# A graph attention kernel: small operands and statistics of its list-making stage moved to PSUM, ScalarE and TensorE, and the order of rows found by a product instead of scatters

## The chip, the cores and the metric

The kernel runs on one core of a Trainium2 chip. The metric is the device time of one execution in microseconds (us), as the median of the runs shown. Engines are named as the profile names them: PE (TensorE), DVE (VectorE), ACT (ScalarE), POOL (GpSimd) and SP (SyncE, which here only issues transfers). SBUF is the memory on which the engines work, PSUM the small memory that PE writes its products to; DVE and ACT read and write both.

## The reference

The input is a matrix x of 3327 rows (nodes) by 1024, and an adjacency matrix of 3327 x 3327 int32 with ones on its diagonal and about 17 ones in a row, at random places.

```
h = relu(layernorm(x))                   # no gain, no bias, eps 1e-5
f = h @ Wf + bf;  g = h @ Wg + bg        # 1024 x 1024 weights, float32
e = relu(f @ g.T)
scores = where(adj > 0, e, -9e15)
out = x + softmax(scores, axis=1) @ (h @ W + bW)
```

## The kernel before

The function `edge_path` does all the work on the usual input; `dense_path` is a fallback behind a flag that is not taken. The rows are cut into NT = 26 tiles of 128, the last of 127. The work has two stages.

**Stage one, the making of lists** (lines 356 to 548, the loop at line 510). For each of the 26 tiles, `edges(t)` turns 128 rows of the adjacency matrix into 128 lists of at most KM = 40 neighbours:

- SP issues the load of the rows into tile `a` (L416; two buffers). ACT copies them to float in `r` and sums each row, which is the degree (L418; two buffers of `r`). POOL multiplies `r` by `iotaj`, the column numbers 1 to 3327 (L419).
- DVE takes the eight largest of each of 16 segments of 208 columns (MAX8, L422) into `cand`, counts them (L424), and draws the 40 largest from `cand` by five MAX8 and four MATCH_REPLACE (L429, L431). The result `lst` is clamped (L432) and written as int32 into its place in `pay` (L433), the table of lists, which has two more columns: the node's own number and its degree `dg` (L435, L436).
- DVE makes `oh`, a one-hot row of the degree over NBIN = 64 bins, by comparing `iotad` with `dg` (L437). For each node PE counts the earlier nodes of the same degree: a strictly triangular matrix `tri` times `oh` for those of the same tile (L439), and a matrix of ones `onesb` times `cum` for those of earlier tiles (L442). `cum` is the running sum of the `oh`, added on DVE (L443). DVE picks each node's own bin from the product (L448); this becomes `rp`.

`normed(t)` normalizes the same rows of x: load on SP (L395), BN_STATS on DVE (L398, L400), the square root on ACT (L402), reciprocal and the product `nmr` on DVE (L403, L405), one ACT pass for scale, shift and relu (L406), and a store of h to `hd` in device memory on SP (L407). Beside it the weights are folded into one matrix A = Wf Wgᵀ: tiles 0 to 7 load and transpose Wg (`load_Wg`, L457, L458), tiles 8 to 15 load and transpose Wf and make eight products of 16 matmuls of 512 columns (`make_A`, L482, 32 records of the trace each), with a bias row (L488). `make_rows` (L490 on), called at tile 16, makes the other bias rows, `v3` and `bW3`, which `split3` (L339) cuts into three bf16 parts on DVE, and the scalar `c_sb`.

After the loop DVE works out each node's rank by falling degree (L522 to L531): a running sum over the bins, a product over 1664 elements (L527), a sum. Then POOL issues 26 indirect scatters, which write the rows of `pay` to `pd` in device memory in the order of rank (L534).

**Stage two, attention** (L551 on), over 26 tiles of rows in the order of rank, so that all rows of a tile have nearly the same degree. `prepare(s)` loads the lists of tile s from `pd` into `pi` (SP, L597), POOL gathers the rows `hp` of h by the column of node numbers (line 599 through the helper at L566), PE transposes them and multiplies by A to `q` (L606), DVE makes the mask from the degrees (L610 to L613) and a bias `ci` (L616). For each neighbour k, POOL gathers the rows `G` of h (L566; 23 buffers) and DVE takes the dot product with `q` (L629). After the softmax, DVE and ACT sum the `G` with the weights into `y` (L667, L669), PE multiplies by W (L684), DVE adds x, gathered by POOL into `xp` (L693), and POOL scatters the rows to the output (L694). The degree cap of each tile (37 falling to 11) sets how many gathers and dots it has.

A scheduler of the framework decides in which order instructions stand on each engine, from its own estimates; every engine then runs its list in that order. A tile's buffers (a pool with `bufs=2`, say) decide how far one step can run ahead of the next.

## Time and profile before

| | before |
|---|---|
| median of 3 runs | 1936.72 us (1935.0 to 1939.14) |
| the profiled execution, own time | 1940.96 us |
| its span (first to last instruction) | 1939.2 us |
| mean granted TensorE clock | 0.803 of full speed |
| DVE busy | 1619.8 us (84%) |
| PE busy | 1069.0 us (55%) |
| POOL busy | 835.1 us (43%) |
| ACT busy | 258.8 us (13%) |

A row of a group of instructions reads: line, engine, operation, output<-input with the partitions x elements and the type, the count, then after the bar the busy time in us and the mean of one in ns, then the engine's idle time just ahead of them with what ended it. A row of a window reads: the stretch, its length, then the busy time of PE, PEld (PE's weight loads), DVE, ACT and POOL with the number of instructions, the granted clock of TensorE, the share of the DMA engines that was busy, and GB/s. A row of the timeline reads: start and duration in us, engine, line, operation, what is made from what, and in brackets the idle time ahead of it with what ended it. A row of the DMA issues reads: what is moved, the queue, the count, the KB of one, and the median time from issue to landing in us. SPq is the transfer queue that SP issues to, POOLq that of POOL.

### The profile page before, as it was taken

Reading aid. Unit: us, or ns where it says so; the run is one execution under the profiler, and the core shown is the slowest. Engines: PE = TensorE matmul, PEld = TensorE weight load, DVE = VectorE, ACT = ScalarE, POOL = GpSimd, SP = SyncE. Lnnn points to the kernel's source line nnn. Section 1 sums busy time; section 2 is a strip of 40 time slices with the busy share of each in tenths; the row PEclk is TensorE's granted clock in tenths of the full one; section 3 lists DMA queues with packets and bytes.
Section 4 is the critical chain, followed back from the end, with each engine's and each line's share of the span. In section 5 each row is a group of like instructions: output and inputs, shape, how many; then the busy total and the mean of one; then the engine's idle time right before and its main releaser. Section 6 shows DMA issues by size and latency. Waiting matters only on the chain.

```text
span 1939.2 us, 11080 instructions
## 1 busy us (share of the span) xinstructions
PE 1069.0 (55%) x2798; PEld 493.0 (25%) x2798; DVE 1619.8 (84%) x2880; ACT 258.8 (13%) x375; POOL 835.1 (43%) x624
## 2 busy tenths in 40 slices
PE   1117775500330472676645566677777678789463
PEld 0113342200110131233222223333333333334221
DVE  7999999634099999999998989889899898887680
ACT  2333434100000110011100000000000001001000
POOL 6445455114433544544335444444354454334610
PEclk9998887755665686887877788888888888899786
DMA  6556566100656857767467656556565565655620
GB/s 228 203 205 247 207 235 228 52 26 30 247 216 202 263 203 241 254 199 222 163 213 249 228 192 227 185 192 238 180 236 222 200 251 200 220 185 195 121 65 13
DMA packets 124618, 372.41 MB, mean 192 GB/s; under 512 B 41210, under 2 KB 41610, under 8 KB 121218
## 3 DMA queue, kind: packets, MB, share of 16 engines
q0 software_dynamic: 106288, 286.93, 43.6%
q1 hardware_dynamic: 18256, 84.68, 11.6%
q8 instruction: 24, 0.39, 0.1%
q14 instruction: 50, 0.40, 0.1%
HBM read 343.64 MB, written 27.81 MB: 192 GB/s over the span
## 4 chain that ended last, share of the span: by engine, by line
issue 24%; DVE 16%; PE 15%; DMA 10%; POOL 8%; ACT 1%; POOLq 0%; SPq 0%; DVEq 0%; ACTq 0%
DVE y L669 13%; PE ps_o L684 11%; POOL G L566 7%; DMA pi<-pd 3%; DMA G<-hd,pi 2%; DMA out_dram<-xp,pi 2%; PE ps_t L577 2%; PE q L606 1%; DMA hp<-hd,pi 1%; DVE junk L629 1%; DMA xp<-in_x_dram,pi 1%; PE ps_o L685 0%; ACT y L667 0%; DVE sc L629 0%; POOL out_dram L694 0%
## 5 line engine op out<-in xcount | busy, mean ns | idle before, releaser
L566 POOL DMA_INDIRECT G<-hd,pi x468 | 512.4, 1095 | 450.0 <-ACT y L667 172.9
L629 DVE CUSTOM_DVE_ANT_0 junk<-G,q,ci 128x1024 bf16<-128x1024 f32 (+1 forms) x468 | 597.7, 1277 | 35.4 <-PE q L607 22.1
L669 DVE SCALAR_TENSOR_TENSOR y<-G,sc,y 128x1024 f32<-128x1024 f32 (+1 forms) x442 | 566.4, 1283 | 26.1 <-ACT y L667 18.7
L684 PE MATMUL ps_o<-W_sb,yT 128*128 128x512 f32 (+1 forms) x832 | 408.4, 648 | 0.8 <-ACT yT L578 0.8
L606 PE MATMUL q<-A_sb,hT 128*128 128x512 f32 (+1 forms) x832 | 372.9, 601 | 7.0 <-ACT hT L578 7.0
L577 PE MATMUL ps_t<-ident,y 128*128 128x128 f32 (+1 forms) x208 | 48.9, 413 | 502.3 <-DVE y L669 283.3
L419 POOL TENSOR_TENSOR r<-r,iotaj 128x3327 f32<-128x3327 f32 (+1 forms) x26 | 187.4, 7209 | 229.8 <-ACT r L418 163.1
L684 PEld LDWEIGHTS ps_o<-W_sb,yT 128*128 128x128 f32 (+1 forms) x832 | 168.9, 209 | 210.2 <-issue 201.9
L606 PEld LDWEIGHTS q<-A_sb,hT 128*128 128x128 f32 (+1 forms) x832 | 154.5, 191 | 194.5 <-issue 180.5
L577 PEld LDWEIGHTS ps_t<-ident,y 128*128 128x128 f32 (+1 forms) x208 | 39.3, 217 | 509.4 <-issue 288.6
L482 PE MATMUL ps_A<-WgT,WfT 128*128 128x512 f32 x256 | 127.2, 660 | 14.6 <-ACT WfT L458 14.6
L694 POOL DMA_INDIRECT out_dram<-xp,pi x26 | 34.0, 1309 | 234.7 <-DVE xp L693 87.4
L439 PE MATMUL ps_pre<-oh,tri 128*128 128x64 bf16 x26 | 5.2, 203 | 230.1 <-DVE oh L437 216.6
L422 DVE MAX8 cand<-r 128x8 f32<-128x208 f32 (+2 forms) x416 | 122.4, 359 | 0.0
L578 ACT COPY yT<-ps_t 128x512 f32<-128x512 f32 (+1 forms) x52 | 30.1, 585 | 564.1 <-PE ps_t L577 563.9
L418 ACT ACTIVATE r<-a 128x3327 f32<-128x3327 int32 (+1 forms) x26 | 77.2, 2968 | 52.2 <-DMA a<-in_adj_dram 52.2
L693 DVE TENSOR_TENSOR xp<-ps_o,xp 128x512 f32<-128x512 f32 (+1 forms) x52 | 35.9, 690 | 47.3 <-PE ps_o L685 47.2
L610 DVE CAST df<-pi 128x1 f32<-128x1 int32 (+1 forms) x26 | 3.9, 150 | 85.2 <-DMA pi<-pd 85.2
L482 PEld LDWEIGHTS ps_A<-WgT,WfT 128*128 128x128 f32 x256 | 53.9, 214 | 82.3 <-issue 66.7
L578 ACT COPY hT<-ps_t 128x512 f32<-128x512 f32 (+1 forms) x52 | 28.0, 588 | 285.9 <-PE ps_t L577 225.0
L577 PE MATMUL ps_t<-ident,hp 128*128 128x128 f32 (+1 forms) x208 | 29.4, 286 | 63.6 <-DMA hp<-hd,pi 63.6
L566 POOL DMA_INDIRECT hp<-hd,pi x26 | 32.9, 1264 | 70.0 <-DMA pi<-pd 48.7
(115 smaller groups left out, 819.3 us busy)
## 6 DMA issues: line engine op xcount, KB each, us to landing
a<-in_adj_dram SPq DMA_DIRECT2D x25, 1663.5 KB, 8.7
xt<-in_x_dram SPq DMA_DIRECT2D x25, 512.0 KB, 4.8
hd<-xt SPq DMA_DIRECT2D x25, 512.0 KB, 3.0
G<-hd,pi POOLq DMA_INDIRECT x468, 5.9
wr<-in_L_gnn_Wg_dram SPq DMA_DIRECT2D x8, 512.0 KB, 7.6
wr<-in_L_gnn_Wf_dram SPq DMA_DIRECT2D x8, 512.0 KB, 5.2
W_sb<-in_L_gnn_W_dram SPq DMA_DIRECT2D x1, 4096.0 KB, 13.0
a<-in_adj_dram SPq DMA_DIRECT2D x1, 1650.5 KB
```

Source lines behind the costliest of these rows:

```text
L418: nc.scalar.activation(r[:n], a[:n], AF.Relu, accum_out=deg[:n, t : t + 1])
L419: nc.gpsimd.tensor_mul(r[:n], r[:n], iotaj[:n])
L422: nc.vector.max(cand[:n, s * 8 : s * 8 + 8], r[:n, s * SW : min(N, (s + 1) * SW)])
L482: nc.tensor.matmul(ps, WfT[:, k, :], WgT[:, k, o * CB : (o + 1) * CB], start=(k == 0), stop=(k == KD - 1))
L566: nc.gpsimd.indirect_dma_start(out=to, out_offset=None, in_=table, in_offset=bass.IndirectOffsetOnAxis(ap=idx, axis=0),)
L577: nc.tensor.transpose(ps[:, k, :n], of[:n, (g + k) * P : (g + k + 1) * P], ident[:n, :n])
L578: nc.scalar.copy(to[:, g : g + 4, :n], ps[:, :, :n])
L606: nc.tensor.matmul(qo, hT[:, k, :n], A_sb[:, k, o * CB : (o + 1) * CB], start=(k == 0), stop=False)
L629: nc.vector.tensor_tensor_reduce(junk[:n], g[:n], e["q"][:n], 1.0, e["ci"][:n], op0=ALU.mult, op1=ALU.add, accum_out=e["sc"][:n, k : k + 1],)
L669: nc.vector.scalar_tensor_tensor(y, G[s, k][:n], p, y, op0=ALU.mult, op1=ALU.add)
L684: nc.tensor.matmul(ps[:n], yT[:, k, :n], W_sb[:, k, o * CB : (o + 1) * CB], start=(k == 0), stop=False)
L693: nc.vector.tensor_add(xo, e["o"][o][:n], xo)
```

## The change

The change touches stage one, and the places where stage two takes the order of rows from. Line numbers here are those of the changed kernel. `p_c` and `p_lst` are pools in PSUM.

1. `iotad` and `lst` are placed in PSUM instead of SBUF.
2. The histogram is kept by PE: one PSUM tile `pre` is accumulated over the whole loop. For each tile PE adds `tri` times `oh` (L461), DVE reads its hit (L463 to L465), and then PE adds `low`, the lower triangle with its diagonal, times `oh` (L466), so that `pre` then holds in all rows the count of all tiles so far. `cum` and its additions go.
3. The statistics of the even tiles' layernorm are taken by ACT in two passes over x that sum (Copy and Square, L417, L421), those of the odd tiles by BN_STATS on DVE as before. `nmr` is made by ACT for all tiles. The stores of h to `hd` are issued by ACT instead of SP.
4. `edges` is cut in two: `degrees(t)` (load, L431, the ACT pass, L433, the POOL product, L434) now stands ahead of `normed(t)`, the rest after it.
5. The lists in `pay` lose the column of node numbers and are stored to `pd` in the order of nodes, in blocks of four tiles by plain stores on ACT's queue (`store_lists`, L471; the block of tiles t-7 to t-4 after tile t). Tiles 20 to 25 are stored after the loop, tile 25 with its 127 rows by a store of its own (L475).
6. After the loop, the rank is split in its low 7 bits and the rest, DVE makes a one-hot of each (`ohp` 128 x 26 x 128, `ohs`), and 26 matmuls add up `perm`: for each rank the number of the node that has it. The 26 scatters go.
7. In stage two `pi` is an indirect gather by POOL from `pd` with `perm` as its index, instead of a load by SP. `hp`, `xp` and the output scatter take their index from `perm` instead of a column of `pi`.
8. `make_rows` is called after the loop instead of at tile 16; its small loads are issued at the start.

```diff
-        iotad = c1.tile([P, NBIN], FP, name="iotad")
+        iotad = p_c.tile([P, NBIN], FP, name="iotad")
+        pre = p_c.tile([P, NBIN], FP, name="pre")
...
+            if t % 2:
...
+                nc.scalar.activation(nmr[:n], mv[:n, 0:1], AF.Copy, scale=-1.0)
+                nc.scalar.activation(rstd[:n], mv[:n, 1:2], AF.Sqrt, bias=eps[:n])
+            else:
+                nc.scalar.activation(j[:n], xt[:n], AF.Copy, accum_out=sums[:n, 0:1])
+                nc.scalar.activation(nmr[:n], sums[:n, 0:1], AF.Copy, scale=-1.0 / D)
+                nc.scalar.activation(j[:n], xt[:n], AF.Square, bias=nmr[:n], accum_out=sums[:n, 1:2])
+                nc.scalar.activation(rstd[:n], sums[:n, 1:2], AF.Sqrt, bias=eps[:n], scale=1.0 / D)
             nc.vector.reciprocal(rstd[:n], rstd[:n])
-            nc.vector.scalar_tensor_tensor(nmr[:n], mv[:n, 0:1], -1.0, rstd[:n], op0=ALU.mult, op1=ALU.mult)
+            nc.scalar.activation(nmr[:n], nmr[:n], AF.Copy, scale=rstd[:n])
             nc.scalar.activation(xt[:n], xt[:n], AF.Relu, bias=nmr[:n], scale=rstd[:n])
-            nc.sync.dma_start(hd[t * P : t * P + n, :], xt[:n])
+            nc.scalar.dma_start(hd[t * P : t * P + n, :], xt[:n])
...
-            lst = cpool.tile([P, KM], FP, name="lst")
+            lst = p_lst.tile([P, KM], FP, name="lst")
...
-            nc.tensor.matmul(ps, tri, oh[:, t, :], start=True, stop=(t == 0))
-                nc.tensor.matmul(ps, onesb, cum[t - 1], start=False, stop=True)
-                nc.vector.tensor_add(new, cum[t - 1], oh[:, t, :])
+            nc.tensor.matmul(pre, tri, oh[:, t, :], start=(t == 0), stop=False, skip_group_check=True)
             nc.vector.scalar_tensor_tensor(
-                hit[:n], ps[:n], 1.0, oh[:n, t, :], op0=ALU.mult, op1=ALU.mult, accum_out=rp[:n, t : t + 1]
+                hit[:n], pre[:n], 1.0, oh[:n, t, :], op0=ALU.mult, op1=ALU.mult, accum_out=rp[:n, t : t + 1]
             )
+            nc.tensor.matmul(pre, low, oh[:, t, :], start=False, stop=(t == NT - 1), skip_group_check=True)
...
         for t in range(NT):
-            edges(t)
+            r = degrees(t)
             normed(t)
+            edges(t, r)
+            if t % 4 == 3 and t > 4:
+                store_lists(t - 7, t - 3)
             if t < KD:
                 load_Wg(t)
             elif t < 2 * KD:
                 make_A(t - KD)
-            elif t == 2 * KD:
-                make_rows()
+        store_lists(20, NT)
...
+        nc.vector.tensor_tensor(
+            ohp, lo[:, :, None].to_broadcast([P, NT, P]), iotap[:, None, :].to_broadcast([P, NT, P]), op=ALU.is_equal
+        )
...
         for t in range(NT):
-            ins = nc.gpsimd.indirect_dma_start(
-                out=pd[:, :],
-                out_offset=bass.IndirectOffsetOnAxis(ap=ranki[:n, t : t + 1], axis=0),
-                in_=pay[:n, t, :],
-                in_offset=None,
-            )
+            nc.tensor.matmul(
+                ps[:, : 2 * NT], ohp[:, t, :], place[:, t, :, :].rearrange("p a s -> p (a s)"),
+                start=(t == 0), stop=(t == NT - 1),
+            )
...
+        nc.vector.scalar_tensor_tensor(perm, ps[:, :NT], float(P), tens, op0=ALU.mult, op1=ALU.add)
+        make_rows()
...
-        nc.sync.dma_start(pi[:n], pd[s * P : s * P + n, :])
-        gather(hp[:n], hd[:, :], pi[:n, KM : KM + 1])
+        gather(pi[:n], pd[:, :], perm[:n, s : s + 1])
+        gather(hp[:n], hd[:, :], perm[:n, s : s + 1])
```

The scheduler orders the instructions anew. The list of PE before, between the third and the fourth of the eight products (L482 is `make_A`'s product, L488 its bias row, L457 the transposes of the next rows of Wf, L439 and L442 the histogram):

```order
L482 MATMUL ps_A<-WgT,WfT 128x512 x16
L488 MATMUL ps_u<-WfT,bgr 128x128 x8
L457 MATMUL ps_tr<-ident,wr 128x128 x8
L439 LDWEIGHTS tri
L439 MATMUL ps_pre<-oh,tri 128x64
L442 LDWEIGHTS onesb
L442 MATMUL ps_pre<-cum,onesb 128x64
L439 LDWEIGHTS tri
L439 MATMUL ps_pre<-oh,tri 128x64
L442 LDWEIGHTS onesb
L442 MATMUL ps_pre<-cum,onesb 128x64
L482 MATMUL ps_A<-WgT,WfT 128x512 x16
```

PE's list there is the product, its bias row, the transposes, and two tiles' histogram matmuls. The same place after the change (L511 is the product, L517 the bias row, L482 now the transposes, L461 and L466 the histogram):

```order
L511 MATMUL ps_A<-WgT,WfT 128x512 x16
L517 MATMUL ps_u<-WfT,bgr 128x128 x8
L482 MATMUL ps_tr<-ident,wr 128x128 x8
L461 LDWEIGHTS tri
L461 MATMUL pre<-oh,tri 128x64
L466 LDWEIGHTS low
L466 MATMUL pre<-oh,low 128x64
L461 LDWEIGHTS tri
L461 MATMUL pre<-oh,tri 128x64
L466 LDWEIGHTS low
L466 MATMUL pre<-oh,low 128x64
L511 MATMUL ps_A<-WgT,WfT 128x512 x16
```

The pattern is the same; `low` stands in the place of `onesb`, and between a tile's two matmuls DVE's hit must be read, since both write the same `pre`.

The list of DVE before, at the last tile of the loop (the tile of 127 rows; L422 draws candidates, L429 and L431 the lists, L398 are the layernorm statistics):

```order
L422 MAX cand<-r 127x8 x7
L436 CAST pay<-dg 127x1
L437 TENSOR_SCALAR oh<-iotad,dg 127x64
L424 TENSOR_SCALAR pos,cnt<-cand 127x128
L429 MAX lst<-cand 127x8
L443 TENSOR_TENSOR cum<-cum,oh 128x64
L448 SCALAR_TENSOR_TENSOR hit,rp<-ps_pre,oh 127x64
L431 MATCH_REPLACE cand<-lst,cand 127x128
L398 BN_STATS st<-xt 127x6
```

The statistics of the last tile stand behind its own candidates. After the change (L443 draws candidates now, L450 and L452 the lists, L410 are the statistics):

```order
L450 MAX lst<-cand 128x8
L410 BN_STATS st<-xt 127x6
L452 MATCH_REPLACE cand<-lst,cand 128x128
L410 BN_STATS st<-xt 127x6
L450 MAX lst<-cand 128x8
L443 MAX cand<-r 128x8
L452 MATCH_REPLACE cand<-lst,cand 128x128
L443 MAX cand<-r 128x8
L450 MAX lst<-cand 128x8
L443 MAX cand<-r 128x8
```

The statistics of the last tile's x now stand ahead of the candidates of the tile before it (rows with 128 partitions are tile 24's or 23's).

The list of POOL before, from the last product of the loop into stage two:

```order
L419 TENSOR_TENSOR r<-r,iotaj 128x3327 x25
L419 TENSOR_TENSOR r<-r,iotaj 127x3327
L534 DMA pd<-pay,ranki 3327x42 x26
L566 DMA hp<-hd,pi 128x1024 x2
L566 DMA G<-hd,pi 128x1024 x23
L566 DMA xp<-in_x_dram,pi 128x1024
```

After the change (L608 is the helper that gathers, L736 the scatter of the output):

```order
L434 TENSOR_TENSOR r<-r,iotaj 128x3327 x25
L434 TENSOR_TENSOR r<-r,iotaj 127x3327
L608 DMA hp<-hd,perm 128x1024 x2
L608 DMA xp<-in_x_dram,perm 128x1024 x2
L608 DMA hp<-hd,perm 128x1024 x2
L608 DMA pi<-pd,perm 128x41 x3
L608 DMA G<-hd,pi 128x1024 x38
L608 DMA pi<-pd,perm 128x41
L608 DMA G<-hd,pi 128x1024 x32
L608 DMA pi<-pd,perm 128x41
L608 DMA G<-hd,pi 128x1024 x3
L736 DMA out_dram<-xp,perm 3327x1024
```

The scatters are gone; gathers of `hp` and `xp` now come first, three gathers of `pi` stand ahead of the first `G`, and each later one stands ahead of some 30 gathers of `G`.

At the end of the loop SP's list was, before: the load of `a` for tile 24, a store of `hd`, a load of `xt`, the load of `a` for tile 25, a store of `hd`, the load of the last `xt`, two stores of `hd`, then W and the 26 loads of `pi`. It now is: two loads of `xt`, the loads of `a` for tiles 24 and 25, the load of the last `xt` (127 rows), and W; the stores of `hd` and of the lists stand on ACT's list behind its passes.

More of the change, by code (lines that the diff above doesn't have):

```diff
@@ L308, in edge_path @@
     SW = -(-N // SEG)
-    PW = KM + 2
+    PW = KM + 1
     def rows(t):
@@ L331, in edge_path @@
     nc.gpsimd.memset(bads, 0.0)
+    perm = const.tile([P, NT], I32, name="perm")
     A_sb = wts.tile([P, KD, D], FP, name="A_sb")
@@ L419, in edges @@
             nc.gpsimd.tensor_mul(r[:n], r[:n], iotaj[:n])
+            return r
+        def edges(t, r):
+            n = rows(t)
             cand = cpool.tile([P, SEG * 8], FP, name="cand")
@@ L491, in make_rows @@
         def make_rows():
-            bf3 = c1.tile([P, KD, 3], FP, name="bf3")
-            nc.vector.tensor_copy(bf3, bfT[:, :, None].to_broadcast([P, KD, 3]))
-            bWf = c1.tile([3, O], FP, name="bWf")
-            nc.gpsimd.dma_start(bWf, bass.AP(tensor=bW.tensor, offset=bW.offset, ap=[[0, 3], [1, O]]))
+            ps = p_u.tile([P, P], FP, name="ps_u")
+            for k in range(KD):
+                nc.tensor.matmul(ps[:, 0:1], bgr[:, k, :], bfT[:, k : k + 1], start=(k == 0), stop=(k == KD - 1))
+            nc.scalar.copy(c_sb, ps[:, 0:1])
             for o in range(OH):
```

96 lines of the change are left out of this document (58 added, 38 removed).

## The prediction

> **What bounds the kernel now.** I read the page first: the span, the share of each engine, and the row of slices. Then windows of stage one and stage two beside each other:
>
> ```profile
> span 1939.2 us, 11080 instructions
> 200.00:250.00 50.00, 41.51 (x128) 21.12 (x127) 49.45 (x161) 21.02 (x25) 28.77 (x4) 0.89 0.63 238
> 600.00:1000.00 400.00, 203.04 (x504) 91.01 (x504) 379.19 (x525) 39.59 (x72) 183.66 (x172) 0.75 0.69 226
> ```
>
> In the loop of lists (200 to 250 us) DVE is busy for 49.45 of 50 us, so it sets the pace; PE with 41.51 is next. In stage two DVE is again full (379.19 of 400) with the dots and sums, which the change leaves alone. So the change is worth what it takes from the time until the first dot, and what DVE waits for afterwards. The timeline tells what DVE's fullness in the loop is made of (start, duration):
>
> ```profile
> 99.23 7.19 POOL L419 TENSOR_TENSOR r<-r,iotaj 128x3327 f32<-128x3327 f32 x1 [5.95 <-ACT r L418]
> 99.88 6.54 DVE L405 SCALAR_TENSOR_TENSOR nmr<-mv,rstd 128x1 f32<-128x1 f32 x1
> 111.86 0.16 DVE L405 SCALAR_TENSOR_TENSOR nmr<-mv,rstd 128x1 f32<-128x1 f32 x1
> 111.94 4.51 DVE L422 MAX8 cand<-r 128x8 f32<-128x208 f32 x16
> 109.14 0.25 DVE L437 TENSOR_SCALAR oh<-iotad,dg 128x64 bf16<-128x64 f32 x1
> 109.99 0.17 DVE L433 TENSOR_SCALAR pay<-lst 128x40 int32<-128x40 f32 x1
> 110.17 0.22 DVE L448 SCALAR_TENSOR_TENSOR hit<-ps_pre,oh 128x64 f32<-128x64 f32 x1
> 418.56 7.19 POOL L419 TENSOR_TENSOR r<-r,iotaj 127x3327 f32<-127x3327 f32 x1 [61.56 <-ACT c_sb L508]
> 418.59 0.67 DVE L343 COPY rest<-ps_A 3x512 f32<-3x512 f32 x1
> 419.38 6.64 DVE L347 CAST part<-rest 3x512 bf16<-3x512 f32 x1
> ```
>
> A one-column product on DVE (L405) takes 0.16 us when POOL is idle, and 6.54 when POOL's product runs: it ends at 106.42, the very moment at which POOL's ends (99.23 + 7.19). The cast at 419.38 likewise ends within 0.3 us of POOL's. But the copy L343, which reads PSUM, took its 0.67 us in the midst of POOL's product. So some DVE operations between SBUF and SBUF are held while POOL works on tensors, and the DVE of the loop is partly busy with being held. The groups of the loop, with the mean in ns behind the busy time:
>
> ```profile
> L419 POOL TENSOR_TENSOR r<-r,iotaj 128x3327 f32<-128x3327 f32 (+1 forms) x26 | 187.4, 7209 | 229.8 <-ACT r L418 163.1 <-ACT c_sb L508 61.6 <-DVE cand L422 5.1
> L405 DVE SCALAR_TENSOR_TENSOR nmr<-mv,rstd 128x1 f32<-128x1 f32 (+1 forms) x26 | 62.1, 2389 | 0.1
> L437 DVE TENSOR_SCALAR oh<-iotad,dg 128x64 bf16<-128x64 f32 (+1 forms) x26 | 28.6, 1102 | 0.0
> L433 DVE TENSOR_SCALAR pay<-lst 128x40 int32<-128x40 f32 (+1 forms) x26 | 17.9, 690 | 0.1
> L443 DVE TENSOR_TENSOR cum<-cum,oh 128x64 bf16<-128x64 bf16 x25 | 20.7, 829 | 0.0
> L398 DVE BATCH_NORM_STATS2 st<-xt 128x6 f32<-128x512 f32 (+1 forms) x52 | 35.1, 679 | 8.0 <-DMA xt<-in_x_dram 8.0
> L482 PE MATMUL ps_A<-WgT,WfT 128*128 128x512 f32 x256 | 127.2, 660 | 14.6 <-ACT WfT L458 14.6
> ```
>
> **The loop, step by step.** The pace before: the ACT pass for tile 0 starts at 12.06 and that for tile 23 at 330.71, so one tile takes 318.65 / 23 = 13.85 us.
>
> ```profile
> 12.06 2.96 ACT L418 ACTIVATE r<-a 128x3327 f32<-128x3327 int32 x1
> 330.71 2.98 ACT L418 ACTIVATE r<-a 128x3327 f32<-128x3327 int32 x1
> 143.41 15.18 PE L482 MATMUL ps_A<-WgT,WfT 128*128 128x512 f32 x32
> 331.05 16.99 PE L482 MATMUL ps_A<-WgT,WfT 128*128 128x512 f32 x32
> 347.60 0.76 SPq L416 DMA_DIRECT2D a<-in_adj_dram  x1
> 415.42 2.98 ACT L418 ACTIVATE r<-a 127x3327 f32<-127x3327 int32 x1 [52.23 <-DMA a<-in_adj_dram]
> ```
>
> What DVE loses: L405 goes to ACT, 62.1 us; L437 with its `iotad` in PSUM falls from 28.6 to 26 x 0.25 = 6.5, saving 22.1; L443 goes, 20.7; L433 reads PSUM, 17.9 - 26 x 0.17 = 13.5; half of L398 goes, 17.5. Together 135.9 us, 5.2 a tile, which leaves DVE 8.6 us a tile. Two other limits lie near: the load side, and PE. By the window at 200, 63% of the DMA engines' time moved 238 GB/s, so full they would move 378; a tile with adjacency rows, x, h and a weight block is 3.2 MB, 8.7 us. For the first eight tiles I take 10 us, above both, for waits in lists that are worked off in order.
>
> From tile 8 on, PE: product and histogram alternate on PE's list, and the lists of later tiles can't pass a product. The eight products start between 143.41 and 331.05, one per 26.8 us. By itself one costs 15.18 to 16.99 us (take 16.1), the bias row 15.6 / 8 = 1.95, eight transposes 1.6: 19.7. With 2.3 us of waits for DVE's hits and ACT's copies I take 22, between 19.7 and the old 26.8.
>
> ```profile
> L488 PE MATMUL ps_u<-WfT,bgr 128*128 128x128 f32 x128 | 15.6, 275 | 0.0
> L457 PE MATMUL ps_tr<-ident,wr 128*128 128x128 f32 x128 | 25.5, 359 | 22.4 <-DMA wr<-in_L_gnn_Wg_dram 20.4 <-DMA wr<-in_L_gnn_Wf_dram 2.0
> ```
>
> Tile 8 is then ready at 12.06 + 8 x 10 = 92, its product can start 10 us later, at 102. The last load, that of tile 25, needs a buffer that the ACT pass of tile 23 frees, and that pass stands on ACT's list behind the copy of the eighth product's first half: 102 + 6.5 x 22 = 245, plus two passes of 2.98 and their waits: the load is issued at about **252**, against 347.60 before. With 19.7 and 8.7 it would be 224, with 26.8 and 10 us it would be 283, with 13.85 us a tile 313.
>
> **The end of the loop.** The load of tile 25 has 127 rows. It was issued at 347.60 and its pass ran at 415.42, so it took 67.8 us; the 25 others took a median of 8.7:
>
> ```profile
> a<-in_adj_dram SPq DMA_DIRECT2D x25, 1663.5 KB, 8.7
> xt<-in_x_dram SPq DMA_DIRECT2D x25, 512.0 KB, 4.8
> 1911.25 2.55 POOL L694 DMA_INDIRECT out_dram<-xp,pi  x1 [34.12 <-DVE flag L739]
> ```
>
> The change keeps this load: it lands at 252 + 67.8 = 320. [...]
>
> Behind that load, on the same queue, stands the last x (127 rows, 508 KB). I scale by bytes: 508 / 1650.5 x 67.8 = 20.9 us after it; ahead of it nothing else can move its DVE and ACT work. Before, its normalization ran during the other waiting. Now its BN_STATS stand ahead of the candidates of tile 24 in DVE's list, so DVE waits there from about 300 on: 20.9 + 9 us for statistics, MAX8 (4.51) and lists makes 30; ACT's sums and relu, 34; then the store of the last h, 127 rows again, 20.9 to 28 us (the last output scatter, of the same size, took 1939.2 - 1911.25 = 28), mean 24.4: the gather of `hp` may go at 320 + 59. The order by product comes to the same time without it: MAX8 4.5 and lists 4.5 for tile 25 after the 30, then the rank 4.4, `ohp` (3328 elements at the rate of L527, 1.886 us for 1664) 3.8, the other one-hots 2.4, 26 matmuls at the 0.2 us of L439 5.3, small ones 2: 57. From `hp`'s gather to the first dot took 534.43 - 511.26 = 23.2:
>
> ```profile
> 511.26 1.00 POOL L566 DMA_INDIRECT hp<-hd,pi  x1 [17.38 <-DVE df L610]
> 534.43 1.28 DVE L629 CUSTOM_DVE_ANT_0 junk<-G,q,ci 128x1024 bf16<-128x1024 f32 x1 [15.19 <-PE q L607]
> L527 DVE TENSOR_TENSOR r<-oh,incl 128x1664 f32<-128x1664 bf16 x1 | 1.9, 1886 | 0.0
> L439 PE MATMUL ps_pre<-oh,tri 128*128 128x64 bf16 x26 | 5.2, 203 | 230.1 <-DVE oh L437 216.6 <-DVE hit L448 13.5
> ```
>
> So the first dot comes at 320 + 82 = **402**, against 534.43: 132 us. Costs put at nothing: `split3`, moved behind `perm`, is some 21 us of DVE, but the first dot waits for the product with A anyway, which ends at +81; were that cover gone, 21 us. The stores of lists on ACT's queue stand behind the last h; the first `pi` gather waits for the 127-row one, at most 59 + 24.4 + 5.9, so 7 us past +82 at worst. [...] The 26 scatters that go are inside the 132: at 0.97 us and 0.30 ahead of each, they held POOL for some 33.
>
> ```profile
> 488.77 0.97 POOL L534 DMA_INDIRECT pd<-pay,ranki  x1 [0.30 <-issue]
> ```
>
> [...] Here L448, which reads PSUM, took 0.22 us, and L437, which doesn't, 0.25: no surcharge shows, and I put it at nothing.
>
> **Stage two.** DVE waits there for the loads of `pi` and once for `hp`:
>
> ```profile
> DVE df L610 <- DMA pi<-pd: 34.5, 14, 4.7
> DVE junk L616 <- DMA hp<-hd,pi: 12.6, 1, 12.6
> L566 POOL DMA_INDIRECT G<-hd,pi x468 | 512.4, 1095 | 450.0 <-ACT y L667 172.9
> G<-hd,pi POOLq DMA_INDIRECT x468, 5.9
> ```
>
> With `hp` and `pi` gathered ahead by an index that lies in SBUF, both waits can go, 47 us at most. POOL gets 26 gathers more at about 0.97 + 0.30 (the last rows of the scatters), 33 us; it idles 450 us ahead of its `G`, which covers it. Some of the waits will only move to `q` and `G`; I take **25**, between 0 and 45.
>
> **Sum:** 132 + 25 = 157. Against its own execution the span falls from 1939.2 to 1782; the profiled execution took 1940.96, 4.2 above the median of 1936.72, and from the median the time is 1936.7 - 157 = **1780 us**. The forecast's own range: the load issued at 224 to 283 and 0 to 45 in stage two give roughly 1740 to 1830.
>
> **The rivals.**
>
> - *The loop keeps its pace.* PE's list or ACT's, in order, holds the loop at 13.85 us a tile, and DVE only waits more. For it: PE is busy 41.51 of 50 us in the window at 200, and ACT gets two more passes over x for every second tile. Against it: the eight products with all that belongs to them fill 19.7 of 26.8 us, and ACT is at 21.02 of 50. Only SP's list gains: the load of tile 25 goes when the pass of tile 23 has ended, 330.71 + 2.98 = 333.7 instead of 347.6, 14 us; the first dot is at 333.7 + 67.8 + 82 = 483.5, 51 us earlier, with 25 makes 1861. Chance 0.12.
> - *Operands in PSUM are held all the same,* so that the change doesn't do what it says. The row for L343 speaks against it (one row, 3 partitions). DVE then keeps most of its load; 1861 again, from the same 51 and 25. Chance 0.03.
> - *Slower: POOL's gathers of `pi` stand in the way of `G`.* If each stopped POOL's list until its data is there, 26 x (0.97 + 0.30 + 5.9) = 186 us, against the 132 that are won, and the 25 not won: 1936.7 - 132 + 186 = 1991. It decides from 132 / 26 = 5.1 us a tile. Against it: each `pi` stands some 30 gathers of `G` ahead of its own first use, and the 23 buffers of `G` keep DVE fed for 23 x 1.28 = 29 us. Chance 0.02.
> - *Faster: the loop falls to POOL's pace,* 7.2 us and half a microsecond of wait, 7.7 a tile: the load of tile 25 goes at about 210, the rest is as above: 1936.7 - (132 + 42) - 25 = 1738. It needs PE's products to fit in 15 us each, which they don't unless the lists run ahead of them. Chance 0.08.
>
> **How the numbers follow.** Forecast 0.75, rivals 0.12, 0.03, 0.02 and 0.08. The likeliest gives 1780. The range reaches from below the fast rival to near the slow loop: 1732 to 1855, which leaves out 0.12 + 0.03 + 0.02 and some of the forecast's edges. A difference within 0.2% (about 4 us) can't be told from none here. Faster by more: all but the slower rival and a little, 0.97; the same, 0.01; slower, 0.02.
>
> **What the profile afterwards would show.** Right: the group of `nmr` gone from DVE, L437 and L433's successors near 0.2 us each, an ACT pass per tile every 10 to 11 us, the 127-row load issued near 252 and landing 68 us later, the first dot near 402, DVE's waits for `pi` gone. Wrong: the load issued after 310 (the loop's pace, and then whichever engine is full in the window at 200), one-hot rows of 1 us mean (PSUM held), DVE waits on `G` behind POOL's `pi` rows in stage two, or a first dot more than 100 us behind the load's landing (the tail).

## The result and the profile after

The changed kernel takes **1795.18 us** (median of 4 runs, 1793.09 to 1797.43) against 1937.2 (4 runs, 1935.0 to 1939.14): a ratio of 0.9267, 95% interval 0.9251 to 0.9283. The forecast was 1780, with a range of 1732 to 1855. The profiled execution took 1794.12, its span is 1792.4.

The windows of the changed kernel (columns as before: length, then busy time of PE, PEld, DVE, ACT and POOL, granted clock, DMA share, GB/s):

```profile
150.00:200.00 50.00, 45.13 (x141) 22.80 (x141) 41.34 (x207) 38.18 (x58) 42.58 (x6) 0.97 0.89 327
200.00:250.00 50.00, 40.82 (x132) 21.25 (x131) 37.62 (x182) 29.43 (x46) 25.42 (x4) 0.86 0.69 248
300.00:350.00 50.00, 5.72 (x12) 0.63 (x11) 9.40 (x46) 6.94 (x11) 7.19 (x1) 0.50 0.07 30
500.00:900.00 400.00, 224.49 (x558) 101.19 (x559) 376.47 (x528) 41.68 (x75) 185.95 (x175) 0.77 0.67 218
```

In the loop DVE is no longer full (37.62 to 41.34 of 50), and no other engine is either (PE, the busiest, 40.82 to 45.13): that is a loop of waits between lists that are worked off in order. The empty stretch, 300 to 350, is as empty as the one before the change, only earlier. The groups of the loop (mean in ns behind the busy time, then idle time and who ended it):

```profile
L458 DVE TENSOR_SCALAR oh<-iotad,dg 128x64 bf16<-128x64 f32 (+1 forms) x26 | 7.1, 274 | 0.0
L454 DVE TENSOR_SCALAR pay<-lst 128x40 int32<-128x40 f32 (+1 forms) x26 | 4.7, 182 | 0.0
L453 DVE TENSOR_SCALAR lst<-lst 128x40 f32<-128x40 f32 (+1 forms) x26 | 4.9, 190 | 0.0
L443 DVE MAX8 cand<-r 128x8 f32<-128x208 f32 (+2 forms) x416 | 134.0, 360 | 47.9 <-POOL r L434 47.9
L410 DVE BATCH_NORM_STATS2 st<-xt 128x6 f32<-128x512 f32 (+1 forms) x26 | 17.7, 680 | 69.2 <-DMA xt<-in_x_dram 69.2
```

The one-hot rows and the int32 lists run at 0.27 and 0.18 us, whatever POOL does (the longest single ones took 0.28 and 0.20). DVE now waits for POOL (47.9 us), and once, for 69.2 us, for the last x. The ACT pass of tile 8, and the first, the sixth and the last of the eight products show the pace (start, duration):

```profile
89.55 2.96 ACT L433 ACTIVATE r<-a 128x3327 f32<-128x3327 int32 x1
95.85 2.05 PE L511 MATMUL ps_A<-WgT,WfT 128*128 128x512 f32 x2
208.73 16.58 PE L511 MATMUL ps_A<-WgT,WfT 128*128 128x512 f32 x32
252.43 14.00 PE L511 MATMUL ps_A<-WgT,WfT 128*128 128x512 f32 x32 [0.28 <-ACT WfT L483]
```

The products start 22.4 us apart on average ((252.43 - 95.85) / 7). The timeline from the last loads to the first dot (start, duration, in brackets the wait):

```profile
246.18 3.35 SPq L431 DMA_DIRECT2D a<-in_adj_dram  x2
318.58 2.98 ACT L433 ACTIVATE r<-a 127x3327 f32<-127x3327 int32 x1 [54.65 <-DMA a<-in_adj_dram]
338.40 0.69 DVE L410 BATCH_NORM_STATS2 st<-xt 127x6 f32<-127x512 f32 x1 [69.22 <-DMA xt<-in_x_dram]
376.04 1.25 POOL L608 DMA_INDIRECT hp<-hd,perm  x1 [47.12 <-issue]
390.60 0.67 DVE L343 COPY rest<-ps_A 3x512 f32<-3x512 f32 x1
391.41 8.83 PE L648 MATMUL q<-A_sb,hT 128*128 128x512 f32 x16 [6.64 <-DVE rest L343]
401.30 0.42 DVE L354 CAST bW<-part_acc 3x512 bf16<-3x512 f32 x1
401.98 0.95 POOL L608 DMA_INDIRECT pi<-pd,perm  x1 [15.80 <-DVE bW L354]
416.27 1.28 DVE L671 CUSTOM_DVE_ANT_0 junk<-G,q,ci 128x1024 bf16<-128x1024 f32 x1 [5.61 <-DMA G<-hd,pi]
```

The last adjacency load goes at 249 (the second of the two issues that end at 249.53) and lands at 318.58; the last x lands 19.8 us behind it; `hp` is gathered at 376.04; the first dot stands at 416.27, against 534.43 before: 118.2 us won. From there to the end it is 1376.1 us against 1404.8: 28.7 won. Together 146.8, the whole difference of the spans. DVE's waits in stage two that stand for the second part:

```profile
DVE df L652 <- DMA pi<-pd,perm: 11.9, 9, 4.7
DVE junk L671 <- DMA G<-hd,pi: 20.7, 11, 7.4
```

### The profile page after: what moved, and what is told of

The parts are those of the page before. It is cut to its first block, busy times and chain, and to the rows that moved or that the text cites. A ratio compares the mean times of both kernels' runs of the same rounds, so it can differ in the third digit from the quotient of the medians.

```text
span 1792.4 us, 10947 instructions
## 1 busy us (share of the span) xinstructions
PE 1069.6 (60%) x2824; PEld 493.0 (28%) x2824; DVE 1478.6 (82%) x2798; ACT 296.9 (17%) x480; POOL 827.9 (46%) x625
## 4 chain that ended last, share of the span: by engine, by line
DVE 27%; PE 27%; issue 22%; POOL 9%; DMA 7%; another core or an unknown queue 4%; ACT 2%; POOLq 0%; ACTq 0%; DVEq 0%
DVE y L711 15%; PE ps_o L726 14%; PE q L648 8%; POOL r L434 5%; DVE junk L671 5%; DMA G<-hd,pi 4%; POOL G L608 3%; DVE cand L443 2%; PE ps_A L511 2%; PE ps_t L619 2%; DMA hd<-xt 1%; ACT r L433 1%; DVE sc L671 1%; DVE lst L450 1%
## 5 line engine op out<-in xcount | busy, mean ns | idle before, releaser
L608 POOL DMA_INDIRECT G<-hd,pi x468 | 505.2, 1080 | 418.8 <-DVE y L711 163.3
L726 PE MATMUL ps_o<-W_sb,yT 128*128 128x512 f32 (+1 forms) x832 | 402.6, 640 | 1.3 <-ACT yT L620 1.3
L648 PE MATMUL q<-A_sb,hT 128*128 128x512 f32 (+1 forms) x832 | 372.6, 601 | 14.1 <-ACT hT L620 7.5
L434 POOL TENSOR_TENSOR r<-r,iotaj 128x3327 f32<-128x3327 f32 (+1 forms) x26 | 188.3, 7250 | 131.8 <-ACT r L433 127.4
L443 DVE MAX8 cand<-r 128x8 f32<-128x208 f32 (+2 forms) x416 | 134.0, 360 | 47.9 <-POOL r L434 47.9
L511 PE MATMUL ps_A<-WgT,WfT 128*128 128x512 f32 x256 | 126.3, 655 | 0.5 <-ACT WfT L483 0.5
L608 POOL DMA_INDIRECT hp<-hd,perm x26 | 27.8, 1068 | 172.0 <-PE ps_t L619 118.7
L433 ACT ACTIVATE r<-a 128x3327 f32<-128x3327 int32 (+1 forms) x26 | 77.1, 2967 | 56.4 <-DMA a<-in_adj_dram 54.7
L608 POOL DMA_INDIRECT xp<-in_x_dram,perm x26 | 34.6, 1329 | 94.7 <-DMA out_dram<-xp,perm 83.1
L410 DVE BATCH_NORM_STATS2 st<-xt 128x6 f32<-128x512 f32 (+1 forms) x26 | 17.7, 680 | 69.2 <-DMA xt<-in_x_dram 69.2
L511 PEld LDWEIGHTS ps_A<-WgT,WfT 128*128 128x128 f32 x256 | 53.0, 211 | 76.6 <-issue 68.4
L687 ACT ACTIVATE sc<-sc,nm 128x11 f32<-128x11 f32 (+11 forms) x32 | 9.8, 308 | 372.6 <-DVE nm L683 272.6
L736 POOL DMA_INDIRECT out_dram<-xp,perm x26 | 31.8, 1222 | 74.0 <-DVE rs L696 34.0
L466 PE MATMUL pre<-oh,low 128*128 128x64 bf16 x26 | 5.4, 207 | 101.5 <-DVE hit L463 101.5
```

The source lines that it names most:

```text
L433: nc.scalar.activation(r[:n], a[:n], AF.Relu, accum_out=deg[:n, t : t + 1])
L434: nc.gpsimd.tensor_mul(r[:n], r[:n], iotaj[:n])
L443: nc.vector.max(cand[:n, s * 8 : s * 8 + 8], r[:n, s * SW : min(N, (s + 1) * SW)])
L511: nc.tensor.matmul(ps, WfT[:, k, :], WgT[:, k, o * CB : (o + 1) * CB], start=(k == 0), stop=(k == KD - 1))
L608: nc.gpsimd.indirect_dma_start(out=to, out_offset=None, in_=table, in_offset=bass.IndirectOffsetOnAxis(ap=idx, axis=0),)
L648: nc.tensor.matmul(qo, hT[:, k, :n], A_sb[:, k, o * CB : (o + 1) * CB], start=(k == 0), stop=False)
```

## The experiments

Each experiment was timed beside the kernel before on the same chip, whose median there was between 1939 and 1942. "+" and "-" in us against the changed kernel are worked out from the ratios, times 1937.2.

**1. Both small operands back in SBUF** (the changed kernel).

```diff
-        iotad = p_c.tile([P, NBIN], FP, name="iotad")
+        iotad = c1.tile([P, NBIN], FP, name="iotad")
...
-            lst = p_lst.tile([P, KM], FP, name="lst")
+            lst = cpool.tile([P, KM], FP, name="lst")
```

> The changed kernel with the two small operands (the bins' numbers and the list) back in SBUF; all else stays. Theory, that DVE operations between SBUF and SBUF are held while POOL's product runs and those with a PSUM operand are not: the one-hot row goes from 0.27 us mean back to about 1.1, the int32 list from 0.18 to about 0.7, the clamp from 0.19 to about 0.46, together 26 x 1.6 = 42 us more of DVE in the loop; DVE has some 20% to spare there, so about half of it shows: 10 to 25 us longer. Rival, that the place of the operands does not matter and the relief came from the operations that left DVE: means stay at 0.2 to 0.3 us and the time within 5 us.

Measured: 1856.51 us, ratio 0.9568 (0.955 to 0.9586), +58, far more than expected. The loop's groups of this kernel, and its window:

```profile
L452 DVE TENSOR_SCALAR lst<-lst 128x40 f32<-128x40 f32 (+1 forms) x26 | 64.2, 2469 | 0.1
L457 DVE TENSOR_SCALAR oh<-iotad,dg 128x64 bf16<-128x64 f32 (+1 forms) x26 | 46.1, 1774 | 0.0
L453 DVE TENSOR_SCALAR pay<-lst 128x40 int32<-128x40 f32 (+1 forms) x26 | 24.6, 948 | 0.1
```

```profile
150.00:200.00 50.00, 43.22 (x156) 23.63 (x154) 49.59 (x155) 26.93 (x39) 28.88 (x4) 0.97 0.60 233
```

In the kernel before the clamp had been:

```profile
L432 DVE TENSOR_SCALAR lst<-lst 128x40 f32<-128x40 f32 (+1 forms) x26 | 11.9, 459 | 0.0
```

The operations are held again, but not with the means they had before the change: the clamp takes 2.47 us instead of 0.46. `nmr`, which had been caught for 2.39, is no longer there. Above their means in PSUM (0.19, 0.27, 0.18) the three come to 59 + 39 + 20 = 118 us, about as much as the five groups of before above 0.2 us each (`nmr`, one-hot, `cum`, list and clamp, 115). DVE is full again (49.59 of 50). So for these three the place of the operands decides, and a hold that was taken from one operation fell on the next (the clamp, from 0.46 to 2.47). Not every small operation in SBUF is held, though: the reciprocals (`rstd`), `dg` and its cast into `pay` read and write SBUF too, and their means stayed between 0.12 and 0.16 us before, after and in experiments 1 to 5, 7, 8 and 12. What sets them apart was not tested.

**2. The kernel before with the operands in PSUM and `nmr` on ACT**, nothing else. The edit in words: `iotad` copied to a PSUM tile, `lst` in PSUM, `nmr` by the two ACT passes of the change, one buffer less for the bias row and the histogram.

```diff
-            nc.vector.scalar_tensor_tensor(nmr[:n], mv[:n, 0:1], -1.0, rstd[:n], op0=ALU.mult, op1=ALU.mult)
+            nc.scalar.activation(nmr[:n], mv[:n, 0:1], AF.Copy, scale=-1.0)
+            nc.scalar.activation(nmr[:n], nmr[:n], AF.Copy, scale=rstd[:n])
```

> The kernel before with one part of the change alone: the two small operands in PSUM, and the product of mean and scale on ACT. Theory: DVE loses 62 + 22 + 13.5 + 7 = 104 us of holding in the loop, which then runs at about 10 us a tile instead of 13.85, until PE and the load side limit it; the load of the last tile is issued 50 to 80 us earlier and the time falls by as much, 50 to 80 us. Rival, that another engine or the order of the lists holds the loop: not more than 20 us.

Measured: 1910.79 us (1899.96 to 1917.44), ratio 0.9839 (0.9795 to 0.9884): 31 us less than before (22 to 40 by the interval), below the theory's 50 to 80 and above the rival's 20. Its loop shows why:

```profile
L448 DVE TENSOR_TENSOR cum<-cum,oh 128x64 bf16<-128x64 bf16 x25 | 87.4, 3497 | 0.0
```

The running sum `cum`, 0.83 us before, now takes 3.5: of the operations made for every tile it is the only one still held. The theory of holds stood, its sum by operation fell. I formed it anew: a hold lasts as long as one operation in a tile can be caught. The next two runs test that.

**3. Only the bins' numbers back in SBUF** (the changed kernel, first hunk of experiment 1).

> The changed kernel with one small operand, the bins' numbers, back in SBUF; the list stays in PSUM. Theory, that the time for which DVE is held is kept as long as one operation that can be held stands in a tile: the one-hot row alone takes up most of the hold, 2 to 4 us mean against 0.27, and the time grows by 35 to 60 us, nearly as with both operands in SBUF (61 us). Rival, that holds add up by operation: the mean goes to about 1.1 us as in the kernel before, 22 us of DVE in all, and the time grows by 5 to 25 us.

Measured: 1837.79 us, ratio 0.9476 (0.9458 to 0.9494), +40; the rival's 5 to 25 is excluded.

```profile
L458 DVE TENSOR_SCALAR oh<-iotad,dg 128x64 bf16<-128x64 f32 (+1 forms) x26 | 87.9, 3382 | 0.0
```

One operation that can be held costs 81 us of DVE (3.38 against 0.27 us), three cost 118. So the hold is not quite kept: each further operation catches what the first let through.

**4. Experiment 2 with the histogram kept by TensorE**, so that `cum` goes too.

```diff
-            nc.tensor.matmul(ps, tri, oh[:, t, :], start=True, stop=(t == 0))
...
-                nc.vector.tensor_add(new, cum[t - 1], oh[:, t, :])
...
+            nc.tensor.matmul(pre, tri, oh[:, t, :], start=(t == 0), stop=False, skip_group_check=True)
...
+            nc.tensor.matmul(pre, low, oh[:, t, :], start=False, stop=(t == NT - 1), skip_group_check=True)
```

> The kernel before with the two small operands in PSUM, the product of mean and scale on ACT, and the histogram kept by TensorE, so that the running sum leaves DVE; statistics on DVE, stores of h on SP and the scatters stay. Theory of the kept hold: with the last operation gone that can be held (it had taken up 3.5 us a tile in the run without this step), the loop runs at 9 to 10.5 us a tile and the load of the last tile is issued at 250 to 275, against 315 without this step: 40 to 65 us less than that run, 1845 to 1875. Rival, that the rest of the loop's gain came from the statistics and the stores on ACT: within 20 us of that run, 1890 to 1915.

Measured: 1844.78 us, ratio 0.9502 (0.9485 to 0.952): 65 us less than experiment 2 by the ratios, 97 less than before. The last adjacency load goes at 265 (before: 347.6, experiment 2: 315.5):

```profile
265.33 0.33 SPq L421 DMA_DIRECT2D a<-in_adj_dram  x1
331.90 2.98 ACT L423 ACTIVATE r<-a 127x3327 f32<-127x3327 int32 x1 [63.71 <-DMA a<-in_adj_dram]
```

So the gain of the loop needs the operands in PSUM and the histogram on PE together (experiments 1 to 3 each lack a part of this), and these two with `nmr` on ACT, without statistics on ACT, bring most of it: the last load goes 82 us earlier than before, against 98 in the changed kernel. Whether `nmr` had to leave DVE as well was not tested by itself.

**5. Statistics on DVE for all tiles** (the changed kernel).

```diff
-            if t % 2:
+            if True:
```

> The changed kernel with the layernorm statistics of all tiles on DVE again (BN_STATS), none on ACT. Theory, that the loop of the changed kernel is not bound by DVE any more (38 to 42 of 50 us busy): 17.7 us more of DVE fit into its free time, and the time stays within 6 us. Rival, that DVE's work still sets the pace of the loop: 10 to 18 us slower.

Measured: 1764.81 us, ratio 0.911 (0.909 to 0.913): **30 us faster** than the changed kernel, outside both expectations. The loop of this kernel, its first and last product and its last adjacency load, and DVE's wait for POOL (20 to 240 us):

```profile
150.00:200.00 50.00, 48.00 (x175) 25.93 (x174) 49.46 (x243) 34.95 (x51) 40.76 (x7) 1.00 0.94 356
```

```profile
92.42 6.83 PE L511 MATMUL ps_A<-WgT,WfT 128*128 128x512 f32 x14
215.41 14.00 PE L511 MATMUL ps_A<-WgT,WfT 128*128 128x512 f32 x32 [0.22 <-ACT WfT L483]
223.22 0.30 SPq L431 DMA_DIRECT2D a<-in_adj_dram  x1
```

```profile
DVE cand L443 <- POOL r L434: 5.3, 1, 5.3
```

PE and DVE are both full (48.00 and 49.46), products follow each other every 17.6 us ((215.41 - 92.42) / 7) instead of 22.4, the last load goes at 223 instead of 249. (The DMA engines are busy for 0.94 of that window too, so the run doesn't tell which of the three would bind next.) So the statistics on ACT, part of this change, cost 30 us. The waits show the way it goes. Among the products, PE waits for DVE's hits, first in the changed kernel (95.8 to 252.4 us), then in this one (92.4 to 215.4):

```profile
PE pre L466 <- DVE hit L463: 24.1, 8, 5.0
PE pre L466 <- DVE hit L463: 1.4, 4, 0.4
```

In the changed kernel DVE waits for POOL's product (40.9 us from 20 to 240, against the 5.3 above), POOL for ACT's pass over the adjacency rows (63.9 against 49.0), and ACT's list for DVE's reciprocal, for aggregates and for the product with A (20.8, 3.4 and nothing in this kernel),

```profile
ACT nmr L424 <- DVE rstd L423: 31.6, 14, 5.8
ACT nmr L413 <- DVE mv L412: 17.8, 6, 4.2
ACT A_sb L514 <- PE ps_A L511: 11.9, 8, 5.7
```

while the pass for the next tile stands behind. Whether the two passes themselves or the order that they bring do this was not told apart.

**6. Stores of h on SP again** (the changed kernel).

```diff
-            nc.scalar.dma_start(hd[t * P : t * P + n, :], xt[:n])
+            nc.sync.dma_start(hd[t * P : t * P + n, :], xt[:n])
```

> The changed kernel with the stores of h issued by SP again instead of ACT. Theory, that SP works off its list in order, so that a store, which waits for ACT's relu, keeps the loads behind it waiting: the load of the last tile is issued 5 to 20 us later and the time grows by 5 to 20 us. Rival, that the loads were far enough ahead: within 3 us.

Measured: 1823.22 us, ratio 0.9405 (0.9387 to 0.9423), +27, more than the theory's upper end. SP's list waits for ACT's relu (20 to 240 us), and the last load goes at 290 instead of 249:

```profile
SPq L426 <- ACT xt L425: 167.5, 18, 13.1
```

```profile
289.98 0.33 SPq L431 DMA_DIRECT2D a<-in_adj_dram  x1
```

**7. The order of rows by scatters again** (the changed kernel): the one-hots, the 26 matmuls and the stores by blocks go, the 26 scatters, SP's loads of `pi` and the column of node numbers come back.

```diff
-        gather(pi[:n], pd[:, :], perm[:n, s : s + 1])
-        gather(hp[:n], hd[:, :], perm[:n, s : s + 1])
+        nc.sync.dma_start(pi[:n], pd[s * P : s * P + n, :])
+        gather(hp[:n], hd[:, :], pi[:n, KM : KM + 1])
```

> The changed kernel with the order of rows found as before: 26 scatters of the lists by rank, and the lists of a tile loaded by SP in a row. Theory, that the order by product is worth what the scatters hold: they run from about 365 to 398, the first lists are there at about 407 and the first dot comes at about 431 instead of 416 (it no longer waits for the three-part split then), and in stage two the waits for the lists come back: 30 to 45 us slower in all. Rival, that the store of the last h, which lands 10 us after the ranks, hides the scatters: only stage two's share, 10 to 28 us slower.

Measured: 1834.17 us, ratio 0.9453 (0.9437 to 0.9469), +36, as the theory had it. The scatters run from 352.58 to 388, `hp` is gathered at 405.64, the first dot stands at 428.05:

```profile
352.58 1.14 POOL L557 DMA_INDIRECT pd<-pay,ranki  x1 [32.29 <-DVE ranki L553]
385.75 2.57 POOL L557 DMA_INDIRECT pd<-pay,ranki  x1 [0.30 <-issue]
405.64 1.00 POOL L590 DMA_INDIRECT hp<-hd,pi  x1 [17.32 <-DVE df L634]
428.05 1.28 DVE L653 CUSTOM_DVE_ANT_0 junk<-G,q,ci 128x1024 bf16<-128x1024 f32 x1 [14.14 <-issue]
```

That is 12 us later than with the product, although this kernel's last load landed 9 us earlier (309.96), and 25.6 us more behind the first dot (1401.7 to the end against 1376.1).

**8. The bias rows at tile 16 again** (the changed kernel).

```diff
+            elif t == 2 * KD:
+                make_rows()
...
-        make_rows()
```

> The changed kernel with the bias rows made at tile 16 of the loop again, instead of behind the order of rows. Theory, that the split into three parts stands on the path to the first dot (the product with A waited 6.6 us for its copies, the gather of the lists 15.8 us for its last one): the first dot comes 10 to 16 us earlier and the time falls by 8 to 16 us. Rival, that in the loop the same work is paid for in PE's list and in DVE operations that are held: within 5 us, or slower.

Measured: 1800.1 us, ratio 0.9285 (0.9263 to 0.9307): no gain, the theory's 8 to 16 did not come. The split stood in DVE's list not in the loop but between the lists of the last two tiles, behind the wait for x, and the order of rows came later by as much (`perm` lets POOL go at 388.70, not 376):

```profile
388.70 1.09 POOL L609 DMA_INDIRECT pi<-pd,perm  x1 [59.66 <-DVE perm L585]
416.12 1.28 DVE L672 CUSTOM_DVE_ANT_0 junk<-G,q,ci 128x1024 bf16<-128x1024 f32 x1 [13.17 <-PE q L650]
```

So the run did not take the split off the path but moved it to another place there: `hp` was gathered 14 us later than in the changed kernel (390.09), and the first dot stood 26.0 us behind it instead of 40.2. What the split costs inside the loop, experiment 12 tells.

**9 and 10. The last tile's transfers cut into 112 and 15 rows,** in the changed kernel and in the one before (there x, adjacency and h).

```diff
-            nc.sync.dma_start(a[:n], adj[t * P : t * P + n, :])
+            for b, e in pieces(n):
+                nc.sync.dma_start(a[b:e], adj[t * P + b : t * P + e, :])
```

> The changed kernel with each transfer of the last tile's 127 rows (adjacency, x, h, lists) cut into one of 112 rows and one of 15. Theory, that 127 rows are moved by one DMA engine: the adjacency load takes about 10 us instead of 69.5, that of x and the store of h about 5 instead of 20; DVE does not stand still for 69 us before the last tiles; the first dot comes 60 to 75 us earlier (then DVE's lists and the rank set it), and the time falls by 60 to 75 us. Rival, that the load is long for its place in the queue or for a lack of bandwidth: within 5 us.

> The kernel before with the same cut of the last tile's transfers. Theory: the load takes about 10 us instead of 67.8; what is left behind it is DVE's own arrears, which the windows put at about half of the 100 us from 350 to 450: the time falls by 35 to 60 us. Rival as for the cut of the changed kernel: within 5 us.

Measured: 1721.87 us, ratio 0.8877 (0.8858 to 0.8896), -76 against the changed kernel; and 1889.64, ratio 0.9739 (0.972 to 0.9759), 51 less than before. The first lies at the upper end of what the theory had, the second within it. The loads of the first of the two kernels, its last pass and its first dot:

```profile
a<-in_adj_dram SPq DMA_DIRECT2D x1, 1455.6 KB, 10.5
a<-in_adj_dram SPq DMA_DIRECT2D x1, 194.9 KB, 10.6
```

```profile
268.91 2.98 ACT L439 ACTIVATE r<-a 127x3327 f32<-127x3327 int32 x1 [2.56 <-issue]
344.27 1.28 DVE L678 CUSTOM_DVE_ANT_0 junk<-G,q,ci 128x1024 bf16<-128x1024 f32 x1 [5.59 <-DMA G<-hd,pi]
```

The same bytes take 10.6 us instead of 69.4; the pass waits for nothing of note. In the kernel before the same cut is worth 51 us; why it is less there was not tested.

**11. The last tile's gathers with 128 rows and its scatter cut,** on top of 9. The 128th lane reads a row whose results are not stored.

```diff
-        gather(g[:n], hd[:, :], e["pi"][:n, k : k + 1])
+        gather(g, hd[:, :], e["pi"][:, k : k + 1])
```

> The changed kernel with the cut transfers, and in stage two the last tile's gathers made with 128 rows (the last lane reads a row that is not used) and its output scatter cut into 112 and 15. Theory, that the one-engine transfer holds for POOL's queue too (gathers of 127 rows take POOL 2.5 us of issue against 0.94, and the last scatter 28 us to the end): DVE's waits for the last tile's rows and most of the end's 28 us go, 30 to 50 us less than with the cut in stage one alone, 1672 to 1692. Rival, that these gathers are split by rows of their own accord and only the last scatter is long: 15 to 25 us less.

Measured: 1686.86 us, ratio 0.8707 (0.869 to 0.8724): 33 less than experiment 9. A gather of the last tile in experiment 9, and after it one of this kernel with its last scatter:

```profile
1614.30 2.53 POOL L615 DMA_INDIRECT G<-hd,pi  x1 [0.30 <-DVE y L718]
```

```profile
1588.32 0.94 POOL L619 DMA_INDIRECT G<-hd,pi  x1 [0.30 <-issue]
1671.69 0.95 POOL L748 DMA_INDIRECT out_dram<-xp,perm  x1 [26.13 <-DVE flag L793]
```

The last eight had been issued in 2.53 to 3.47 us each and now are in 0.93 to 1.02; the last scatter starts 12 us before the end of the span (1684.0) instead of 28 (1690.45 of 1718.2).

**12. The bias rows at tile 8,** on top of 11.

```diff
+                if t == KD:
+                    make_rows()
                 make_A(t - KD)
...
-        make_rows()
```

> That kernel, and the bias rows made at tile 8 of the loop, ahead of the first product with A, so that their split into three parts stands in DVE's list among the lists of tile 8 to 10. Theory, that the split stands on the path behind the order of rows (its last copy let the gathers of the lists go 26 us after the order was there) and costs the loop less, since DVE has a fifth of it free: 5 to 15 us less than without. Rival, that some 48 operations between SBUF and SBUF in the loop are held by POOL's products and cost as much there: within 4 us, or slower.

Measured: **1682.45 us** (1681.07 to 1684.98), ratio 0.8682 (0.8662 to 0.8701), 4.4 less than 11 in the same comparison: just at the border of theory and rival. The first dot comes 5.8 us earlier (336.69 against 342.49), and stands 27.1 us behind the gather of `hp` (309.58) instead of 40.5 (301.97), but the order of rows is ready 5.6 us later (307.23 against 301.68). So the split is paid for in part in the loop: its first product takes 2.1 us each, against 0.47 behind the loop.

```profile
336.69 1.28 DVE L683 CUSTOM_DVE_ANT_0 junk<-G,q,ci 128x1024 bf16<-128x1024 f32 x1 [14.50 <-issue]
L352 DVE TENSOR_SCALAR part_acc<-part,sel 3x512 f32<-3x512 bf16 x4 | 8.5, 2131 | 0.0
```

This is the fastest of the runs; statistics on DVE (experiment 5) were not tried on top of it.

## Why the prediction was right, and where its steps were off

- **What DVE loses.** DVE's busy time fell by 141 us (1619.8 to 1478.6), 136 had been worked out. That the two agree so closely is in part luck: rows that the sum left out fell by 23 us (the clamp 7.0, the first copy of `cum` 7.1, the split's casts 6.1, the aggregates 2.6), while the MAX8 of the candidates grew by 11.6 and the new one-hots and their sums added 6. And the listed rows, which came out as forecast, do so only because the change takes *every* operation that can be held out of the loop: experiments 1 to 4 show that a part of it would have been worth less than its rows (31 us from four of the five groups, whose rows came to 104).
- **10 us a tile, then 22 us a product.** Measured 9.95 (tile 8's pass starts at 89.55, tile 0's at 9.98) and 22.4 ((252.43 - 95.85) / 7); the load was forecast for 252 and went at 249. The working holds as well: a product by itself took 16.1 us (113.0 / 7), as taken, and PE waited for DVE's hits, 3.4 us a product (24.1 / 7), where I had taken 2.3 for hits and copies together. What I had wrong is where those waits come from. In experiment 5, without ACT's statistics, PE waited 1.4 us in all for hits, a product took 14.1 (99.0 / 7), they followed each other every 17.6, 17.0 of it PE's own work (119.27 / 7), and the load went at 223, where I had put the lower end, 224. So a part of the change that I counted as a saving of 17.5 us on DVE cost 30 us.
- **The 127-row load** took 69.4 us (67.8 forecast), the x behind it 19.8 (20.9), and `hp` was gathered 57.5 us after the landing (59). The order of rows was ready at 53.8 (57), and the store of the last h had been issued 23.3 us before that gather (24.4). The profile names no releaser there, but in experiments 9 and 11, where the store is cut, `hp` goes 0.3 us after the order. Experiments 9 to 11 show the cause: the number of rows. The pieces of 112 and 15 rows took 10.5 and 10.6 us. While the load of 127 rows ran alone, from 280 to 318 us in the changed kernel, the share of the DMA engines was 0.06, about what one of the 16 makes, at 27 GB/s; the two windows of the loop above have 0.69 and 0.89, 248 and 327 GB/s.
- **From `hp` to the first dot: the step that failed.** I took 23.2 us and put `split3` at nothing, since the product with A would cover it. It took 40.2: the product itself waited 6.6 us for a copy of the split (L343, whose source is in the PSUM that the product takes over), and the gather of the lists waited for the split's last cast (L354), which ended 29 us after the order of rows was there (372.36 to 401.72). I had named the price, 21 us; the stretch came out 17 too long. Experiments 8 and 12, which have the split elsewhere, shorten it to 26.0 and 27.1 us, so 13 to 14 of the 17 go with the split; the rest was not looked into. That memory is what ties the product and the gather to the split is read from the program, whose second stage takes over the memory of the first (the data of neither comes from what it waited for), and was not tested. The first dot came at 416 instead of 402.
- **Stage two** gave 28.7 us (25 forecast). Most of DVE's waits for the lists went (34.5 to 11.9 us) and the one for `hp` (12.6); waits for `G` grew from 4.7 to 20.7, as the forecast allowed for. What it had not seen is that DVE's waits for the product with W fell too, from 47.2 to 31.0 us, so that the size owes something to luck. Experiment 7 puts stage two's share of the new order at about 26 us.
- **The sum:** the first dot was put 14 us too early, stage two gave 4 more than taken, and 5 come from the two profiled executions, which stood 3.8 above and 1.1 below their medians: 14 - 4 + 5 = 15 us, the miss of the forecast.
- **PSUM as a source:** a small surcharge shows, which I had put at nothing: by their medians, which leave the holds out, the clamp went from 0.170 to 0.188 us, the cast of the list from 0.168 to 0.182, the one-hot from 0.244 to 0.275. That is 14 to 31 ns each and 1.6 us in 26 tiles.
- **The rivals.** A loop at the old pace: 9.95 us a tile speak against it. PSUM held all the same: 0.27 against 3.38 us (experiment 3). The loop at POOL's pace: products 22.4 us apart speak against it. Gathers of `pi` in the way of `G`: DVE's waits for `G` are 20.7 us in all, not 186.

## What to carry to other kernels

Here an operation on DVE that ended when POOL's did was being held (`nmr`: 6.54 us beside POOL's product, 0.16 when POOL was idle); find all operations that the trace shows held and take them all out of the loop, because here the hold moved on to the next one (the clamp from 0.46 to 2.47 us in experiment 1, `cum` from 0.83 to 3.50 in experiment 2). Look at the row count of a transfer before its bytes: here 127 rows cost seven times 128 (69.4 against 9.4 us), and the remedy was to cut it (76 us, experiment 9), or to gather a whole 128 (33 more with the last scatter cut, experiment 11). When work is moved behind a loop, check which memory it lives in: here a product waited 6.6 us and a gather 15.8 for work whose results they don't read; and a unit with time to spare was no free place for work: ACT, busy for 29 to 38 of 50 us in the loop and working off its list in order, took the statistics, and they cost 30 us.

## What the runs showed of the hardware that I had not expected

- The hold depended on the operations that were there: 3.1 us a tile above its own time with one that can be held (81 / 26), 4.5 with three (118 / 26), in a loop with one POOL product of 7.2 us a tile.
- A wait of PE cost more than its length. In the changed kernel the products with A that started at 122.83, 208.73 and 233.08, behind waits of 4.0 to 5.0 us, took 16.35 to 16.86 us; those at 187.73 and 252.43, behind waits of 0.2 and 0.3, took 14.00, and so did all six that ran in one piece in experiment 5, behind at most 0.7. The granted clock over the products was 0.91 in the changed kernel and 1.00 in experiment 5. It didn't follow PE's busy share alone: the kernel before was granted 1.00 from 50 to 100 us with PE busy for 6.62 of 50.
- Indirect gathers and scatters by POOL paid for 127 rows too: in the changed kernel the last eight gathers took 2.52 to 3.47 us to issue, where the median of all is 0.94, and landed 24.9 to 27.7 us after the issue, where the median is 5.9; the scatter of 127 rows in experiment 7 took 2.57 us to issue against 0.97.
